# Sharing the query evacuation between ScalarE and VectorE, and recording the norm's means and the first pointwise layer later for three of four images

## The chip, the cores and the metric

The kernel runs on one core of one Trainium2 chip. The metric is the device time of one execution in microseconds (us). A core has five engines that run side by side and meet through semaphores: TensorE (PE in the profile, its weight loads PEld), VectorE (DVE), ScalarE (ACT), GpSimd (POOL) and SyncE (SP), the last used here to issue copies.

## The reference

The input is four images of 64 x 64 positions with 64 channels, in fp32. Four layers follow one another:

```python
# layer 0: self-attention over the 4096 positions of each image
q, k, v = x @ Wq + bq, x @ Wk + bk, x @ Wv + bv
x = gamma * (softmax(q k^T)^T v) + x
# layer 1: a gated convolution block
y = pw1(layernorm(x))                 # 64 -> 256 channels
y = depthwise3x3(y); y = y1 * y2      # the halves of the channels
y = y * (mean over positions of y, through sca)
x = x + pw2(y) * beta
z = pw3(layernorm(x)); x = x + pw4(z1 * z2) * gamma
# layer 2: attention of each image with itself, without projections
x = softmax(x x^T) x + x              # x.reshape(4, 64, 4096): positions and channels regrouped
# layer 3: attention with 32-channel theta, phi, g, then a batch norm over all images
x = x + batchnorm(softmax(theta phi^T) g @ W)
```

Scores, softmax and products dominate: three times four attention maps of 4096 x 4096.

## The kernel before, in words

All that matters is in `fast_path`. One image is kept as a tile X of 128 partitions by 2048 columns: the lower and the upper 64 partitions hold the 64 channels of the two halves of the positions.

**The stream.** `run` records all instructions in one order, and each engine executes its share in that order. The backbone is the list `items`: 32 items for each image's first attention (`layer0`, one item per 128 queries, images one after another, so item 32b is where image b begins), then items of `layer2` and `layer3`. An item of `layer0` is four steps of one score block (L1085, eight TensorE instructions) and one product block (L1111, eight instructions, of a tile six steps back), with one exp of 128 x 1024 (L1090) on ScalarE per score block. After a tile's four exps VectorE sums and scales (`scale`, L1098 to L1101).

**PSUM slots.** `new_ps` deals out slots of 128 x 1024 in rotation. In `layer0` two slots rotate, in `layer2` three. A block that takes a slot waits until whoever read that slot last is done. Score blocks, projections, norms and pointwise blocks all draw on the same rotation.

**Lanes.** Other work is threaded between the steps. Two lanes, `conv` and `misc`, each hold a queue of generators. After each step of `layer0` both get a tick of 1.8 units, conv first. In `layer2` an item ticks 4.6 units twice. A generator that yields a number is resumed when that many units have passed, so a yield says how much later the next piece is recorded, not how long it lasts. The `conv` lane holds `layer1(b)` from item 32b+34 on, one image after another. The `misc` lane holds `project0(b+1)` from item 32b+16 on, and later `features2`, `close2`, `open3`. The convolution work of an image takes longer than a first attention, so it runs on: that of images 2 and 3 reaches into the second attentions of images 0 and 1.

**`project0`.** For images 1 to 3 (the case "once") two query blocks and two value blocks (L1053) are recorded 3.4 units apart. A query block is eight TensorE instructions (L1027) into one slot: the lower 64 partitions get one 512-column group of each half, the upper 64 partitions the next one. ScalarE evacuates the slot in two instructions of 64 x 1024 (L1035), one for each half of the partitions, adding `bqk`. After each, SP issues a copy (L1039) of the new rows to the other 64 partitions of q.

**`norm`.** It is called twice for each image, before the first pointwise layer and before the second half of the block. It squares x on ScalarE (two ACTIVATEs of 128 x 1024, L1154), yields 4.0, takes means of x and of the squares on TensorE (16 instructions, L1160) into one slot, then on ScalarE and VectorE the variance (L1165, L1166), yields 5.0, then Ln and Exp (L1168, L1169), yields 4.0, spreads the result with eight SP copies (L1173), yields 14.0, and multiplies it into x on VectorE in two pieces (L1181), each followed by a yield of 1.8. What comes next in the lane is the first pointwise block, eight instructions a piece (L1195).

**After the norm.** `layer1` evacuates each pointwise block in two ScalarE instructions into a padded tile (`pad`, L1212), does the nine taps of the depthwise convolution on VectorE (L1226 to L1231), the channel weights (L1248), the second pointwise layer (L1257), its evacuation (L1262), again a norm, and the last two layers (L1195 again, L1274, L1276, L1280, L1281). `features2` transposes an image into one slot (L1295) and evacuates it in two halves, the lower partitions on VectorE and the upper on ScalarE (L1298). `turn` in `layer2` transposes a finished part of the output (L1349), which ScalarE (L1343) and VectorE (L1344) have put together.

Of the kernel before, what the change touches and what calls it, by code (L numbers as in the profile page):

```python
# [9 lines left out]
AF = mybir.ActivationFunctionType  # L10
# [681 lines left out]
def fast_path(ctx: ExitStack, tc: tile.TileContext, a: dict, out: bass.AP, bad):  # L692
    nc = tc.nc
    B, H, W, C = a["x"].shape
# [31 lines left out]
    def new_ps():  # L726
        if turn_of["banks"]:
            if turn_of["bank"] % turn_of["banks"] == turn_of["banks"] - 1:
                turn_of["bank"] += 1
            k = new_bank(), new_bank()  # L730
            return PS[:, 512 * k[0] : 512 * k[0] + 1024]
        s = turn_of["slots"][turn_of["ps"] % len(turn_of["slots"])]
        turn_of["ps"] += 1
        return PS[:, bass.ts(s, 1024)]
# [11 lines left out]
    def new_t(name="t"):  # L746
        return tp.tile([128, 1024], F32, tag="t", name=name)

    def new_big(name):
        return big.tile([128, 4096], F32, tag="big", name=name)  # L750
# [5 lines left out]
    act = nc.scalar.activation  # L756
# [77 lines left out]
    for nm in names64 + names32:  # L834
        n = flat[nm].shape[0]
# [31 lines left out]
    bqk = const.tile([128, 1], F32, name="bqk")  # L867
# [106 lines left out]
    def tok(x, s, j):  # L974
        return x[64 * s : 64 * s + 64, bass.ts(j, 512)]
# [41 lines left out]
    def project0(b):  # L1017
        x, m = X[:, b], im[b]
        m.q = new_big("q")
        m.v = new_big("v")[:, 0:2048].rearrange("p (t c) -> p t c", c=C)  # L1020
        once = ((0, "once"), (0, "v"), (1, "once"), (1, "v"))
        for j, w in once if b else ((0, "q"), (0, "v"), (1, "q"), (2, "q"), (1, "v"), (3, "q")):
            ps = new_ps()
            if w == "once":
                for o in range(2):
                    for s in range(2):
                        mm(  # L1027
                            ps[64 * o : 64 * o + 64, bass.ts(s, 512)], wq[64 * s : 64 * s + 64, 0:64],
                            tok(x, s, 2 * j + o), start=True, stop=True,
                        )  # L1030
                qs = m.q.rearrange("p (s n) -> p s n", s=2)
                for o in range(2):
                    own, other = slice(64 * o, 64 * o + 64), slice(64 - 64 * o, 128 - 64 * o)
                    n = bass.ts(2 * j + o, 512)
                    act(  # L1035
                        qs[own, :, n], ps[own, :].rearrange("p (s n) -> p s n", s=2),
                        AF.Identity, bias=bqk[own, :],
                    )
                    nc.sync.dma_start(out=qs[other, :, n], in_=qs[own, :, n])  # L1039
            elif w == "q":  # L1040
                for o in range(0, 128, 64):
                    for s in range(2):
                        mm(
                            ps[o : o + 64, bass.ts(s, 512)], wq[64 * s : 64 * s + 64, o : o + 64],
                            tok(x, s, j), start=True, stop=True,
                        )
                for s in range(2):
                    nc.vector.tensor_scalar_add(
                        m.q[:, 2048 * s + 512 * j : 2048 * s + 512 * j + 512], ps[:, bass.ts(s, 512)], bqk
                    )  # L1050
            else:
                for i in range(8):
                    mm(ps[:, bass.ts(i, 128)], x[:, bass.ts(8 * j + i, 128)], wv, start=True, stop=True)  # L1053
                for s in range(2):
                    nc.vector.tensor_add(
                        m.v[:, 16 * s + 8 * j : 16 * s + 8 * j + 8, :],
                        ps.rearrange("p (t s c) -> p t s c", s=2, c=C)[:, :, s, :],
                        bv.unsqueeze(1).to_broadcast([128, 8, C]),
                    )
            yield 3.4  # L1060
# [85 lines left out]
            items.append((lambda t=t: item(t), 0.0))  # L1146


    def norm(x, y):


        sq = [new_t("sq"), new_t("sq")]
        for i in range(2):
            act(sq[i], x[:, bass.ts(i, 1024)], AF.Square)  # L1154
        yield 4.0
        ps = new_ps()
        for i, src in enumerate(((x, x), (sq[0], sq[1]))):
            for j in range(4):
                c = 512 * j if i == 0 else 512 * (j % 2)
                mm(  # L1160
                    ps[32 * j : 32 * j + 32, bass.ts(i, 512)], jsel, src[j // 2][:, c : c + 512],
                    start=True, stop=True,
                )
        t = new_t()
        act(t[:, 0:512], ps[:, 0:512], AF.Square)  # L1165
        stt(t[:, 0:512], t[:, 0:512], -1.0, ps[:, 512:1024], ALU.mult, ALU.add)  # L1166
        yield 5.0
        act(t[:, 0:512], t[:, 0:512], AF.Ln, bias=eps1)  # L1168
        act(t[:, 512:1024], t[:, 0:512], AF.Exp, scale=-0.5)  # L1169
        yield 4.0  # L1170
        for j in range(4):
            for h in range(2):
                nc.sync.dma_start(  # L1173
                    out=y[64 * h : 64 * h + 64, bass.ts(j, 512)],
                    in_=t[32 * j + 16 * h : 32 * j + 16 * h + 16, 512:1024]
                    .unsqueeze(1).to_broadcast([16, 4, 512]),
                )
        yield 14.0
        for jp in range(2):
            cols = bass.ts(jp, 1024)  # L1180
            nc.vector.tensor_mul(y[:, cols], y[:, cols], x[:, cols])  # L1181
            yield 1.8

    pad = new_pad()
    nc.gpsimd.memset(pad[:, 0:PW], 0.0)
# [3 lines left out]
    def layer1(b):  # L1189
        x = X[:, b]  # L1190
# [8 lines left out]
                    )  # L1199

        y = xn.tile([128, 2048], F32, tag="xn", name="xn")
        yield from norm(x, y)
        yg = new_big("yg")
        yw = yg.rearrange("c (s q p h) -> c p q s h", s=2, p=2, h=H)
        ysum = sm.tile([128, 8], F32, tag="ysum", name="ysum")
        for r in (1, 0):
            inner = pad[:, PW + 1 : 65 * PW + 1].rearrange("c (p q s h) -> c q p s h", p=2, s=2, h=PW)
            for j in range(4):
                ps = new_ps()
# [8 lines left out]
            for j in range(4):  # L1218
                w0 = 16 * j
                y1 = new_t("y1").rearrange("p (w h) -> p w h", h=H)  # L1220
                for k in range(9):
                    o = (w0 + k % 3) * PW + k // 3
# [24 lines left out]
        ps = new_ps()  # L1247
# [6 lines left out]
        for j in range(4):  # L1254
            ps = new_ps()
# [8 lines left out]
            nc.vector.tensor_add(xs, xs, t[:, 0:512])  # L1264
            yield 3.5
        z = xn.tile([128, 2048], F32, tag="xn", name="xn")
        yield from norm(x, z)
        for j in range(4):
            t, u = new_t(), new_t("u")
            for r in range(2):  # L1270
                ps = new_ps()
# [6 lines left out]
            ps = new_ps()  # L1278
# [323 lines left out]
    for b in range(B):  # L1602
        if b:
            misc_to[len(items)] = True
        layer0(b)
        if b + 1 < B:
            gens = [load_x(i) for i in range(1, B)] if b == 0 else []
            misc_from[32 * b + 16] = gens + [project0(b + 1)]
        conv_from[32 * b + 34] = layer1(b)
# [18 lines left out]
    def run():  # L1628
        nc.scalar.preload_act_table_set("natural_log_exp_and_others")
        fold, loads, first = fold_qk(), load_x(0), project0(0)  # L1630
        next(fold)
        next(loads)
        next(fold)
        next(first)
        next(loads)
        between.append(lambda: next(loads))
        misc.add(first)
        conv_from[3] = setup()
        for i in range(max(max(due) + 1, len(items))):
            if i in misc_to:  # L1640
                misc.drain()
            if i in misc_from:
                misc.add(*misc_from[i])
            if i in conv_from:
                conv.add(conv_from[i])
            us = 1.0
            if i < len(items):
                fn, us = items[i]
                fn()
            for lane in (conv, misc):  # L1650
                lane.tick(us)
            for fn in due.get(i, []):
                fn()
            for lane in (conv, misc):
                lane.tick(us)
# [185 lines left out]
```

## Time and profile before

| What | us |
|---|---|
| median of 7 runs | 2574.38 |
| lowest and highest of them | 2573.50, 2575.95 |
| the profiled execution, its own time | 2573.91 |
| its span in the profile | 2572.1 |
| PE busy | 2535.9 |
| ACT busy | 1774.2 |
| DVE busy | 1128.6 |

A line of a timeline gives the start in us from the beginning of the span, the time from the first start to the last end, the engine, the line of the kernel, the operation, the names of output and input with their shapes, and how many instructions were merged; in brackets stands how long the engine sat idle before it and what released it. A line of the waits gives the waiting engine and line, the engine and line it waited for, then total us, number of times and the longest. The granted TensorE clock was 0.998 of full speed. On TensorE x8 is one block of eight instructions.

### The profile page before, as it was taken

How to read it: one execution, taken by the hardware profiler on the slowest of the kernel's cores; microseconds unless marked ns; L12 is line 12 of the kernel's file. 1: busy time of each engine (PE TensorE's matmuls, PEld its weight loads, DVE VectorE, ACT ScalarE, POOL GpSimd, SP SyncE). 2: the span in 40 equal slices, each digit the busy share in tenths (PEclk: the TensorE clock that was granted, in tenths of full speed). 3: DMA queues.
4: the chain of work that ended last, by engine and by line, in shares of the span. 5: the costliest groups of instructions: out<-in, count | busy, mean ns of one | idle time of the engine just before them, and what ended most of it. 6: DMA issues, size and time to landing. Idle time of an engine off the chain costs nothing.

```text
span 2572.1 us, 55249 instructions
## 1 busy us (share of the span) xinstructions
PE 2535.9 (99%) x24293; PEld 847.2 (33%) x24293; DVE 1128.6 (44%) x1292; ACT 1774.2 (69%) x2888; POOL 93.5 (4%) x142
## 2 busy tenths in 40 slices
PE   9999999999999999999999999999999999999998
PEld 3343333333333336333333321233321233321113
DVE  2010266321763227711772138810058600088996
ACT  4666766667666676666656679856689756579996
POOL 2000000000000000000000001000011000011110
PEclk9999999999999999999999999999999999999999
DMA  3000000001000100010010024310034110054444
GB/s 76 1 18 1 18 18 1 7 12 34 1 1 4 32 18 1 1 34 18 1 34 18 18 48 85 67 34 1 18 70 96 34 34 1 1 123 92 85 92 105
DMA packets 38380, 87.06 MB, mean 34 GB/s; under 512 B 5260, under 2 KB 13685, under 8 KB 38133
## 3 DMA queue, kind: packets, MB, share of 16 engines
q0 software_dynamic: 14528, 50.90, 9.6%
q1 hardware_dynamic: 22853, 30.72, 5.3%
q8 instruction: 192, 3.15, 0.5%
q10 hardware_dynamic: 752, 1.85, 0.2%
q14 instruction: 55, 0.45, 0.1%
HBM read 4.80 MB, written 4.19 MB: 3 GB/s over the span
## 4 chain that ended last, share of the span: by engine, by line
PE 92%; ACT 4%; DVE 3%; issue 1%; DMA 0%; SPq 0%; DVEq 0%; ACTq 0%
PE PS L1336 17%; PE PS L1318 17%; PE PS L1111 17%; PE PS L1085 16%; PE PS L1442 8%; PE PS L1499 8%; DVE tg L1490 3%; PE PS L1195 2%; ACT e L1453 2%; ACT e L1090 1%; PE PS L1053 1%; PE PS L1257 1%; PE PS L1280 1%; PE PS L1160 1%; PE PS L1417 1%
## 5 line engine op out<-in xcount | busy, mean ns | idle before, releaser
L1090 ACT ACTIVATE e<-PS 128x1024 f32<-128x1024 f32 x512 | 523.6, 1023 | 326.1 <-PE PS L1085 283.8
L1326 ACT ACTIVATE e<-PS 128x1024 f32<-128x1024 f32 x512 | 516.7, 1024 | 292.8 <-PE PS L1318 289.6
L1111 PE MATMUL PS<-e,vq 64*64 64x512 f32 x4096 | 539.9, 591 | 0.0
L1085 PE MATMUL PS<-X,q 64*64 64x512 f32 x4096 | 536.5, 590 | 1.8 <-DVE X L969 1.7
L1453 ACT ACTIVATE e<-PS 128x512 f32<-128x512 f32 (+2 forms) x586 | 501.3, 923 | 48.3 <-PE PS L1442 28.2
L1318 PE MATMUL PS<-ko 64*64 64x512 f32 x4096 | 469.7, 591 | 5.4 <-ACT e L1453 2.2
L1336 PE MATMUL PS<-e,X 64*64 64x512 f32 x4096 | 464.1, 591 | 0.0
L1490 DVE TENSOR_TENSOR tg<-tg,e 128x2048 f32<-128x2048 f32 x188 | 430.7, 2291 | 32.9 <-ACT e L1453 17.8
L1228 DVE SCALAR_TENSOR_TENSOR y<-pad,vec,y 128x1024 f32<-128x1024 f32 x240 | 308.1, 1284 | 8.2 <-ACT pad L1212 1.1
L1442 PE MATMUL PS<-tg,ph 32*64 32x512 f32 x4096 | 293.8, 613 | 0.1
L1499 PE MATMUL PS<-e,tg 128*32 128x512 f32 x2048 | 272.5, 604 | 0.0
L1085 PEld LDWEIGHTS PS<-X,q 64*64 64x64 f32 x4096 | 161.3, 133 | 279.2 <-issue 231.8
L1318 PEld LDWEIGHTS PS<-ko 64*64 64x64 f32 x4096 | 156.4, 132 | 293.9 <-issue 200.3
L1111 PEld LDWEIGHTS PS<-e,vq 64*64 64x64 f32 x4096 | 160.8, 133 | 272.7 <-issue 170.9
L1336 PEld LDWEIGHTS PS<-e,X 64*64 64x64 f32 x4096 | 155.4, 133 | 275.1 <-issue 271.9
L1098 DVE TENSOR_REDUCE sums<-zs 128x1 f32<-128x4 f32 x128 | 19.8, 155 | 374.3 <-ACT e L1090 374.2
L1344 DVE TENSOR_TENSOR ph<-ph,PS 128x512 f32<-128x512 f32 x16 | 11.0, 687 | 391.7 <-ACT ph L1343 391.7
L1442 PEld LDWEIGHTS PS<-tg,ph 32*64 32x64 f32 x4096 | 62.9, 129 | 217.5 <-ACT e L1453 185.2
L1499 PEld LDWEIGHTS PS<-e,tg 128*32 128x32 f32 x2048 | 41.5, 108 | 205.6 <-issue 201.6
L1326 ACT ACTIVATION_READ_ACCUMULATOR e<-PS 128x1 f32 x512 | 106.1, 207 | 0.0
L1090 ACT ACTIVATION_READ_ACCUMULATOR e<-PS 128x1 f32 x512 | 99.6, 195 | 0.1
L1470 POOL DMA_DIRECT2D xn<-e x16 | 8.8, 559 | 2139.5 <-PE PS L1442 1504.6
(196 smaller groups left out, 1013.0 us busy)
## 6 DMA issues: line engine op xcount, KB each, us to landing
xn<-e POOLq DMA_DIRECT2D x96, 512.0 KB, 5.1
xn<-t SPq DMA_DIRECT2D x64, 128.0 KB
ph<-tg SPq DMA_DIRECT2D x64, 128.0 KB
ko<-ko SPq DMA_DIRECT2D x16, 256.0 KB
xr<-in_x_dram SPq DMA_DIRECT2D x13, 256.0 KB
q<-q SPq DMA_DIRECT2D x12, 256.0 KB
out_dram<-o SPq DMA_DIRECT2D x7, 256.0 KB
out_dram<-o ACTq DMA_DIRECT2D x2, 512.0 KB
```

Of the source, the lines that this page charges most:

```text
L1085: mm(ps[64 * c : 64 * c + 64, bass.ts(r, 512)], m.q[rows_, 128 * t + 64 * c : 128 * t + 64 * c + 64], x[rows_, bass.ts(g, 512)], start=Tru ...
L1090: act(es[g // 2][:, bass.ts(g % 2, 1024)], ps, AF.Exp, bias=SHIFT0, accum_out=zs[:, g : g + 1],)
L1111: ins = mm(PS[64 * s : 64 * s + 64, 2048 + 512 * j : 2560 + 512 * j], vq[rows_, :], es[j // 2][rows_, k : k + 512], start=t == 0 and i < 2 ...
L1195: mm(ps[o : o + 64, bass.ts(s, 512)], w[64 * s : 64 * s + 64, 128 * r + o : 128 * r + o + 64], tok(src, s, j), start=True, stop=True,)
L1228: stt(y1, win, wt, y1, ALU.mult, ALU.add)
L1318: mm(ps[64 * c : 64 * c + 64, bass.ts(r, 512)], m.ko[rows_, 128 * jb + 64 * c : 128 * jb + 64 * c + 64], m.ko[rows_, bass.ts(2 * ib + r, 5 ...
L1326: act(es[n, jb], ps, AF.Exp, bias=SHIFT2, accum_out=m.zs[:, jb, ib : ib + 1])
L1336: mm(acc[r][64 * c : 64 * c + 64, :], xw[rows_, jb, :], es[n, jb][rows_, bass.ts(c, 512)], start=jb == 0, stop=jb == 31,)
L1442: mm(PS[64 * c : 64 * c + 64, bass.ts(banks[k], 512)], m.ph[32 * k : 32 * k + 32, 128 * mc + 64 * c : 128 * mc + 64 * c + 64], m.th[32 * k ...
L1453: act(e[:, 512 * lo : 512 * k], PS[:, 512 * banks[lo] : 512 * banks[lo] + 512 * (k - lo)], AF.Exp,)
L1490: nc.vector.tensor_add(esum, esum, e)
L1499: mm(st["y"][32 * k : 32 * k + 32, :], m.gx[:, i % 32, :], es[i][:, bass.ts(k, 512)], start=mc == 0, stop=i % 32 == 31,)
```

## The change

Three things are edited. In `project0` the second of the two query evacuations of a slot (upper 64 partitions) is made by VectorE as a `tensor_scalar_add` instead of a ScalarE activation; the first stays on ScalarE. `norm` takes a flag, which is true for images 0, 1 and 2: with it the yield after the squares is 6.0 instead of 4.0, and the yield after the second multiply is 3.6 instead of 1.8. Both calls of `norm` in `layer1` pass the flag. As the lane is a queue, everything behind a longer yield in the `conv` lane is recorded later too, image 3's convolution included.

```diff
                     n = bass.ts(2 * j + o, 512)
-                    act(
-                        qs[own, :, n], ps[own, :].rearrange("p (s n) -> p s n", s=2),
-                        AF.Identity, bias=bqk[own, :],
-                    )
+                    src = ps[own, :].rearrange("p (s n) -> p s n", s=2)
+                    if o:
+                        nc.vector.tensor_scalar_add(qs[own, :, n], src, bqk[own, :])
+                    else:
+                        act(qs[own, :, n], src, AF.Identity, bias=bqk[own, :])
                     nc.sync.dma_start(out=qs[other, :, n], in_=qs[own, :, n])
...
-    def norm(x, y):
+    def norm(x, y, slow):
...
-        yield 4.0
+        yield 6.0 if slow else 4.0
...
             nc.vector.tensor_mul(y[:, cols], y[:, cols], x[:, cols])
-            yield 1.8
+            yield 3.6 if slow and jp else 1.8
...
-        yield from norm(x, y)
+        yield from norm(x, y, b + 1 < B)
...
-        yield from norm(x, z)
+        yield from norm(x, z, b + 1 < B)
```

## The prediction

> **What bounds the kernel.** The page comes first, for the busy shares:
>
> ```profile
> PE 2535.9 (99%) x24293; PEld 847.2 (33%) x24293; DVE 1128.6 (44%) x1292; ACT 1774.2 (69%) x2888; POOL 93.5 (4%) x142
> ```
>
> TensorE sets the time, and the change neither adds nor removes a matmul. Only moments in which TensorE starts late can be won or lost. PE's waits from 140 to 1000 us, where images 1 to 3 are projected and most convolution work is laid into the first attention, are the whole prize there:
>
> ```profile
> PE PS L1160 <- ACT e L1090: 2.9, 4, 0.8
> PE PS L1053 <- ACT q L1035: 1.5, 2, 0.8
> PE PS L1195 <- ACT q L1035: 1.4, 2, 0.8
> PE PS L1195 <- ACT ko L1298: 0.5, 1, 0.5
> ```
>
> As matmul ends are modelled, I measure lateness between starts. Score and product blocks (L1085, L1111) follow each other every 0.86 us. A block of another shape (L1053, L1160, L1280, L1295, L1257, L1349) starts 0.11 us later even when it waits for nothing (383.80 to 384.76), and the block after it is 0.05 late. I count what goes beyond. The timeline at the first norm, and then at the second norm of the same image:
>
> ```profile
> 268.25 2.00 ACT L1154 ACTIVATE sq<-X 128x1024 f32<-128x1024 f32 x2
> 270.14 1.01 ACT L1090 ACTIVATE e<-PS 128x1024 f32<-128x1024 f32 x1
> 271.39 1.07 PE L1160 MATMUL PS<-X,jsel 128*32 128x512 f32 x8 [0.84 <-ACT e L1090]
> ```
>
> ```profile
> 498.92 1.99 ACT L1154 ACTIVATE sq<-X 128x1024 f32<-128x1024 f32 x2
> 500.81 1.01 ACT L1090 ACTIVATE e<-PS 128x1024 f32<-128x1024 f32 x1
> 501.97 1.09 PE L1085 MATMUL PS<-X,q 64*64 64x512 f32 x8
> 502.99 1.06 PE L1160 MATMUL PS<-X,jsel 128*32 128x512 f32 x8
> ```
>
> Two squares hold ScalarE for 2 us, so the next exp is late, and the mean matmuls need the PSUM slot that this exp empties. At 271.39 they stand two score blocks behind the squares and lose 1.02-0.11=0.91 us. At 502.99 they stand three behind, as it fell out there, and lose 0.05, with 0.02 at the score before. At 589, 822 and 915 (two behind) the loss is 0.76, 0.77 and 0.77: 3.25 us over five norms.
>
> The query evacuation of image 2:
>
> ```profile
> 370.74 2.23 ACT L1035 ACTIVATE q<-PS,bqk 64x1024 f32<-64x1024 f32 x2
> 372.99 1.02 ACT L1090 ACTIVATE e<-PS 128x1024 f32<-128x1024 f32 x1
> 373.02 2.05 PE L1053 MATMUL PS<-wv,X 128*128 128x128 f32 x16 [0.84 <-ACT q L1035]
> ```
>
> The score block before L1053 began at 371.14; 371.14+0.86+0.11=372.11 was due, so 0.91 is lost. So measured, the six evacuations cost: image 1 twice 0.11 at a score and 0.29 at L1053; image 2 0.91 and 0.97; image 3 0.56 at L1027, which follows L1195 with no product between, then 0.72 and 1.00. Sum 4.96 us.
>
> **The precedent.** The kernel already shares one evacuation between the engines, the transposes of `features2` (L1298):
>
> ```profile
> 870.37 1.22 DVE L1298 COPY ko<-PS 64x1024 f32<-64x1024 f32 x1 [5.69 <-PE PS L1295]
> 871.62 1.01 ACT L1298 COPY ko<-PS 64x1024 f32<-64x1024 f32 x1 [1.20 <-DVE ko L1298]
> 872.68 1.09 PE L1195 MATMUL PS<-xn,pw 64*64 64x512 f32 x8 [0.54 <-ACT ko L1298]
> ```
>
> The halves lie on different partitions, yet ScalarE starts 0.03 us after VectorE ends: one after the other, not side by side.
>
> **What the Trainium skill says.** "PSUM — Partial Sum Buffer", PSUM bank collisions: two engines must not touch one bank and 32-partition quadrant at once, reads included, while different quadrants may be; guarding by whole bank is the simple version. The trace agrees with the simple version here. The same page, Engine vs sequencer instructions: ScalarE's and VectorE's queues are strict FIFO; the exp at 270.14 behind the squares agrees. "Perfetto Trace Analysis", Tensor Engine Instruction: the end of a matmul is estimated, hence starts.
>
> **Part 1, evacuations.** Six ScalarE instructions of 1.11 us (L1035, half of twelve) go; six VectorE ones of the form 64x1024 out of PSUM come, 1.22 us each by the L1298 row (tensor_scalar is priced by that copy; L1048's 0.75 us for 512 columns would bound it at 1.5). In the built order of the changed kernel the VectorE half waits for ScalarE's semaphore alone, not TensorE's: it starts when ScalarE's half ends. The slot is free after 1.11+0.03+1.22=2.36 instead of 2.23 us, 0.13 later, while ScalarE is free 1.12 us earlier for the next exp. The SP queue's four copies per image wait 0.13 longer; queries are needed 13 or more items (about 90 us) later.
>
> Event by event, on the new TensorE order. Image 1: score, which takes the query slot, 0.10+0.13=0.23 late, then L1053 on time, since its exp no longer stands behind the second half: 0.40 becomes 0.23, twice. Image 2, first: the order is unchanged, 0.91 becomes 1.04. Second: the first pointwise block has moved out, two blocks and a product more now stand between, and the score that takes the slot, due at 381.92, finds it free at 382.10: 0.97 becomes 0.23. Image 3: L1195 no longer precedes L1027, so 0.56 goes; 0.72 becomes 1.04 (image 2's pattern), 1.00 becomes 1.13. Sum 3.90, gain 1.06 us. If L1298 underprices VectorE by 0.28, six are later by that: gain -0.6.
>
> Behind the waiting VectorE instruction stand the sums of the score tile (L1098 to L1101, 0.6 us) and taps of the convolution (1.28 us). In image 2 the sums move from 369.10 to 373.1; their vq is first used by a product at about 376.9, 3 us later. Taps need 4x1.28+0.6=5.7 of the 6.9 us that a tile takes; the two tiles with evacuations carry at most 5.7+1.3+1.2=8.2, a lag of some 2.6 us that the next tiles absorb. TensorE waits for the taps only at L1248, once per image.
>
> **Part 2, norms recorded later.** Six norms of images 0 to 2 get 2.0 more after the squares and 1.8 more before the first pointwise block. The new order has three or four exps between squares and mean matmuls in the five norms within the first attention. Three cost 0.07 (502.99); I take 0.07 for four as well. 3.25 becomes 0.35: gain 2.9 us (2.2 if the squares cost 0.2 at each). The sixth (1117) has no loss before. The later pointwise block itself waits for nothing of the norm in the trace before: its multiplies (L1181) at 290.7 and 291.8 precede the block at 297.3. That edit costs nothing, hidden by the score blocks between, and only moves the lane. DMAs of the norm (64, SP) move with it; none is passed by an issue that is late.
>
> **Part 3, all later convolution work moves** by 3.8 per norm, up to 23 lane units at the end. In the first attention one clash arises: L1195 then L1295 without a product at item 112, where the transposes wait for an exp: 0.42, then about 0.15. Before, this region lost 0.61, 0.19 and 0.13. One more shape change costs 0.16: gain 0.2.
>
> From 1000 to 1455 us four scores run in a row, and an evacuation just ahead of such a run delays its exps. Before: one pad pair ahead costs 0.2 (1027, 1214, 1223), two 0.75 (1282), transposes ahead 1.24 and 1.02 (1128, 1442), a norm's Ln and Exp behind the ph copy 0.63 (1198): 4.2 us. In the new order: one double pad 0.75; four single pads 0.8; an output block and transposes ahead 1.6 (VectorE and ScalarE halves in a row hold the third slot until 5.1 us after the product run, due 3.8; the exps give 0.3 more); two pointwise blocks and transposes ahead 1.6 by the same count; small ones 0.15; the Ln and Exp meet no ph copy: 0. Sum 4.9, loss 0.7. Three shape changes merge (L1257 with L1295 twice, with L1349 once), 3x0.16=0.5 back: loss 0.2 (range 1.7 loss to 1.2 gain). The lane ends some 15 us later than 1452 in the second attention, before the next stage takes over at about 1505, so nothing beyond is touched.
>
> **Sum** against the profiled execution (span 2572.1, its own time 2573.91, 1.8 around it): 1.06+2.9+0.2-0.2=4.0 us. Because small late starts round against me, I take 3.7. The span becomes 2568.4. The profiled execution is 0.5 under the median of the runs, 2574.38, so the median becomes 2570.7, 0.14% faster.
>
> **Rivals.** *Side by side*: the halves overlap, no wait between engines. Then the slot is free after about 1.2 us, and of 4.96 some 0.3 stays: 3.6 us more, 2567.1. For it: different partitions; against it: the 0.03 us handover at 871.6 and the built waits. *Given back in the second attention*: the moved lane meets score runs worse than counted, 2.5 us lost: 2573.2. For it: 1.24 us for one clash before; against: the clashes are few. *Slower*: VectorE's half stands behind taps at 48 and 80, so TensorE waits on slots held by a tap queue. To end 0.2% slower (5.1 us) four evacuations must lose 3.7+5.1=8.8 us, 2.2 each, nearly two taps; 2580. Against: taps wait only for pad, run ahead, and idle is what stands before VectorE's evacuations (4.16 us before L1055 at 375.18).
>
> **How the numbers follow.** Likeliest 0.65 (2569.3 to 2572.5), side by side 0.12, given back 0.17, slower 0.06. Of the likeliest, 0.11 reaches beyond 0.2% (5.1 us, below 2569.2; about what a measurement here can tell). Faster 0.11+0.12=0.23, slower 0.06, within 0.71. The range 2567.6 to 2574.2 leaves out the slower case and tails of the outer two.
>
> **What would show it.** Right: L1160's waits in the first attention fall from 2.9 to under 0.5 us; VectorE's query rows begin within 0.1 us of ScalarE's end; L1053 of images 2 and 3 still waits about 0.9 us, now for VectorE. Wrong: both query rows starting together (side by side), VectorE's late behind taps (slower), or late starts between 1000 and 1470 us adding to over 6 us (given back).

## The result, and the profile after

| | before | after |
|---|---|---|
| median, us (runs) | 2574.49 (34) | 2581.54 (14) |
| lowest and highest | 2573.20, 2578.57 | 2580.17, 2583.29 |
| profiled execution: own time, span | 2573.91, 2572.1 | 2579.98, 2578.2 |

The ratio is 1.0027, with a 95% interval of 1.0020 to 1.0033: the change makes the kernel 7 us slower, where 3.7 us faster had been forecast. Lines of the kernel after stand one higher than before from L1039 on; L1037 is VectorE's half of a query evacuation, L1039 ScalarE's.

The page of the kernel after: the busy shares, and of part 4 the shares of the chain that ended last.

```profile
PE 2539.5 (98%) x24293; PEld 846.3 (33%) x24293; DVE 1136.7 (44%) x1298; ACT 1766.5 (69%) x2882; POOL 93.5 (4%) x142
...
PE 89%; DVE 6%; ACT 3%; issue 1%; DMA 0%; SPq 0%; POOL 0%; DVEq 0%; ACTq 0%
```

Six instructions went from ScalarE to VectorE, as meant, and every engine does what it did. But VectorE has 6% of the chain; before it had 3%, and TensorE 92%. TensorE waits somewhere for VectorE where it did not.

To find the place I added up late starts: from every TensorE block to the next, the excess over the usual start-to-start time of such a block, counted where it passes 0.1 us. (The shape changes of 0.11 and 0.16 are in these sums; the prediction had taken them off.)

| Late starts, us | to 135 | first attention, 135 to 994 | second attention of images 0 and 1, from 994 to the first block of layer 3 after them (1513 before, 1518 after) | rest | sum | span |
|---|---|---|---|---|---|---|
| before | 4.7 | 13.5 | 9.2 | 22.3 | 49.8 | 2572.1 |
| after | 5.9 | 9.5 | 17.6 | 23.1 | 56.2 | 2578.2 |

The sums differ by 6.4, the spans by 6.1: the account of the profiled execution is nearly complete. That execution took less than any of the 14 timed runs (2579.98 against a median of 2581.54), so about 1 of the 7 us lost is in no profile. The first attention won 4.0, where 4.16 had been worked out (1.06 + 2.9 + 0.2). The second lost 8.4, where 0.2 had been. The outer columns differ by 1.2 and 0.8; over all kernels here they vary from 4.7 to 5.9 and from 22.3 to 25.1, in no order that follows the edits. The rest, the last stretch of the kernel, follows the clock, as the last section shows.

The first attention first. PE's waits of the kernel after, from 140 to 1000 us:

```profile
PE PS L1054 <- DVE q L1037: 2.0, 2, 1.0
PE PS L1196 <- DVE q L1037: 1.0, 1, 1.0
PE PS L1296 <- ACT e L1091: 0.4, 1, 0.4
```

The norms' 2.9 us (L1160 before) are gone. What stays is the wait for a query slot, and now it is VectorE that holds it. The timeline at image 2's first query evacuation:

```profile
371.18 1.10 ACT L1039 ACTIVATE q<-PS,bqk 64x1024 f32<-64x1024 f32 x1
...
372.31 1.29 DVE L1037 TENSOR_SCALAR q<-PS,bqk 64x1024 f32<-64x1024 f32 x1 [4.22 <-ACT q L1039]
...
373.65 0.60 PE L1054 MATMUL PS<-wv,X 128*128 128x128 f32 x3 [1.02 <-DVE q L1037]
```

VectorE had been idle for 4.22 us, and starts 0.03 us after ScalarE's end (371.18 + 1.10 = 372.28), released by it, as the bracket says. The halves run one after the other, and the slot is free 2.42 us after the first began, 0.19 later than the 2.23 before.

Now the second attention. PE's waits of the kernel after from 1000 to 1470 us; before, this list held L1298 for 1.1 us and an exp for 0.4:

```profile
PE PS L1319 <- DVE tg L1397: 4.3, 1, 4.3
PE PS L1319 <- ACT ko L1299: 1.9, 2, 1.0
PE PS L1319 <- ACT e L1327: 1.0, 1, 1.0
PE PS L1393 <- DVE X L1373: 0.2, 1, 0.2
```

The first line is a wait that the kernel before did not have. It happens once. The timeline of the kernel after around it:

```profile
1284.40 1.91 PE L1393 MATMUL PS<-X,thw 64*32 64x512 f32 x12
...
1286.51 1.05 PE L1393 MATMUL PS<-X,thw 64*32 64x512 f32 x4 [0.20 <-DVE X L1373]
1287.49 1.95 PE L1319 MATMUL PS<-ko 64*64 64x512 f32 x16
1287.70 0.81 DVE L1227 TENSOR_SCALAR y<-pad,vec 128x1024 f32<-128x1024 f32 x1
1288.54 3.92 DVE L1229 SCALAR_TENSOR_TENSOR y<-pad,vec,y 128x1024 f32<-128x1024 f32 x3
...
1292.38 1.28 DVE L1397 TENSOR_SCALAR tg<-PS,vec 128x1024 f32<-128x1024 f32 x1
...
1293.72 3.33 PE L1319 MATMUL PS<-ko 64*64 64x512 f32 x16 [4.28 <-DVE tg L1397]
```

The theta matmuls of image 0 (L1393, in `open3`) fill a slot, and VectorE is to empty it into `tg` (L1397). But VectorE executes in order, and ahead of it stand taps of image 3's convolution (L1227, L1229: 0.81 and 3.92 us). The evacuation starts 4.89 us after the score block that follows the theta matmuls (1287.49 to 1292.38), and the third score block of the run, which takes the slot, starts at 1293.72 instead of 1289.26, two halves of a block after 1288.40. The kernel before at the same point:

```profile
1293.61 3.67 PE L1318 MATMUL PS<-ko 64*64 64x512 f32 x32
1293.82 1.28 DVE L1396 TENSOR_SCALAR tg<-PS,vec 128x1024 f32<-128x1024 f32 x1 [7.35 <-PE PS L1392]
...
1295.02 0.80 DVE L1226 TENSOR_SCALAR y<-pad,vec 128x1024 f32<-128x1024 f32 x1
```

There such taps came just after theta: VectorE stood idle for 7.35 us and began to empty the slot 0.21 us after the first score block had begun, and the four score blocks ran through. The order of these two on VectorE's queue was turned round by the lane that moved.

One more part of the cost is seen in the same place. After the wait the 16 matmuls take 3.33 us, twice the 1.7 of two score blocks. The table of stretches of the kernel after (stretch, length, busy time and count of PE, PEld, DVE, ACT and POOL, then the granted TensorE clock, DMA share, GB/s):

```profile
1288.00:1290.00 2.00, 1.44 (x16) 0.28 (x8) 1.93 (x3) 1.29 (x3) 0.00 (x0) 1.00 0.00 0
...
1294.00:1296.00 2.00, 2.00 (x12) 0.51 (x11) 1.97 (x2) 0.23 (x1) 0.00 (x0) 0.50 0.00 0
...
1297.00:1298.00 1.00, 1.00 (x21) 0.16 (x17) 0.50 (x1) 0.88 (x1) 0.00 (x0) 1.00 0.00 0
```

The clock stood at half in the stretch after the wait. The page "TensorE: Matmul & The Clock Gate" of the Trainium skill, What's actually happening, says that TensorE's clock falls to half after an idle window of about 3.4 us and returns after about as long a busy one. The trace agrees: 4.9 us passed between two starts, and then four groups of matmuls started 0.91, 0.85 and 0.85 us apart where 0.43 is usual. So the block that waited was 4.46 us late, and the first block after the run 6.0 (1296.98 instead of 1288.40 + 3 x 0.86 = 1290.98): a wait of 4.5 cost 6.

### The profile page after: what moved, and what is told of

It reads as the page before. It is cut to its first block, busy times and chain, and to the rows that moved or that the text cites. A ratio compares the mean times of both kernels' runs of the same rounds, so it can differ in the third digit from the quotient of the medians.

```text
span 2578.2 us, 55243 instructions
## 1 busy us (share of the span) xinstructions
PE 2539.5 (98%) x24293; PEld 846.3 (33%) x24293; DVE 1136.7 (44%) x1298; ACT 1766.5 (69%) x2882; POOL 93.5 (4%) x142
## 4 chain that ended last, share of the span: by engine, by line
PE 89%; DVE 6%; ACT 3%; issue 1%; DMA 0%; SPq 0%; POOL 0%; DVEq 0%; ACTq 0%
PE PS L1112 17%; PE PS L1086 17%; PE PS L1337 17%; PE PS L1319 16%; PE PS L1443 8%; PE PS L1500 7%; DVE tg L1491 3%; PE PS L1196 2%; ACT e L1454 2%; DVE y L1229 1%; PE PS L1054 1%; PE PS L1281 1%; PE PS L1258 1%; PE PS L1161 1%; PE PS L1418 1%
## 5 line engine op out<-in xcount | busy, mean ns | idle before, releaser
L1327 ACT ACTIVATE e<-PS 128x1024 f32<-128x1024 f32 x512 | 516.7, 1024 | 301.4 <-PE PS L1319 298.2
L1229 DVE SCALAR_TENSOR_TENSOR y<-pad,vec,y 128x1024 f32<-128x1024 f32 x240 | 308.0, 1283 | 10.2 <-ACT pad L1213 3.2
```

Source lines behind the costliest of these rows:

```text
L1229: stt(y1, win, wt, y1, ALU.mult, ALU.add)
L1327: act(es[n, jb], ps, AF.Exp, bias=SHIFT2, accum_out=m.zs[:, jb, ib : ib + 1])
```

## Experiments

Three theories. **A**: the loss is image 0's theta evacuation, which the moved lane put behind image 3's taps on VectorE. **B**: VectorE's half of the query evacuation costs it, directly or through what is queued behind. **C**: many small clashes of the moved lane with score runs add up. Each kernel was timed beside the kernel before on its own chip, whose medians were 2574.45, 2574.91 and 2574.30 in the three sets; ratios are against these.

### The change in two: the query evacuation alone, the norms alone

The first has the query edit and the yields of before, the second the two longer yields and the evacuation of before.

```diff
+                    if o:
+                        nc.vector.tensor_scalar_add(qs[own, :, n], src, bqk[own, :])
+                    else:
+                        act(qs[own, :, n], src, AF.Identity, bias=bqk[own, :])
```

> Kernel before with the shared query evacuation alone. Theory A (the loss of 7 us comes from theta's evacuation in open3 of image 0 standing behind image 3's taps on VectorE, because the longer yields moved the taps there): the lane is not moved, theta's evacuation stands where it was, so about the time of before, 2573.5 to 2576 us, and the wait of the score block for theta is absent. Theory B (the VectorE half of the query evacuation itself costs the 7 us, through slots held longer): 2579 us or more. Theory C (the many small clashes of moved convolution work with score runs, none dominant): as A, 2573.5 to 2576.

> Kernel before with the longer yields alone, both query halves on ScalarE. Theory A and C: the loss is all here, 2579 to 2582 us, with the score block of the second attention waiting some 4 us for theta's evacuation. Theory B: faster than before by the norm's 2.9 us, about 2571.5 us.

The query edit alone: 2575.84, ratio 1.0005 (0.9996 to 1.0013), no difference that can be told. Late starts in the first attention 14.2 against 13.5, in the second 9.3 against 9.2. The norms alone: 2579.81, ratio 1.0019 (1.0011 to 1.0027); late starts 9.1 and 18.9, and this among PE's waits from 1000 to 1470 us:

```profile
PE PS L1318 <- DVE tg L1396: 4.3, 1, 4.3
```

B falls: the wait and the loss come with the yields alone, and without the query edit. The query edit gains nothing alone.

### Theta of image 0 on ScalarE

The kernel after with one evacuation moved off VectorE.

```diff
-        nc.vector.tensor_scalar_add(m.th, ps, V("L3_conv_theta_b"))
+        act(m.th, ps, AF.Identity, bias=V("L3_conv_theta_b")) if b == 0 else nc.vector.tensor_scalar_add(m.th, ps, V("L3_conv_theta_b"))
```

> Changed kernel with image 0's theta evacuation moved from VectorE to ScalarE, where no taps stand in the queue; nothing else differs. Theory A: 5 to 6 us come back, 2575.5 to 2577 us, and the wait of 4.3 us is gone. Theory C: at most 2 us come back, 2579.5 us or more. Theory B: no change, 2581 us.

2574.27, ratio 0.9996 (0.9988 to 1.0005): 7.3 us below the kernel after by the medians, 4.6 by the profiled spans (its profiled run took 2575.45, the most of its 13), and late starts of the second attention down from 17.6 to 11.8. The timeline there:

```profile
1287.19 3.66 PE L1319 MATMUL PS<-ko 64*64 64x512 f32 x32
1287.31 1.12 ACT L1397 ACTIVATE tg<-PS,vec 128x1024 f32<-128x1024 f32 x1 [4.88 <-PE PS L1393]
1287.40 0.80 DVE L1227 TENSOR_SCALAR y<-pad,vec 128x1024 f32<-128x1024 f32 x1
```

The same taps stand on VectorE at the same time, and the four score blocks run through in 3.66 us. A holds: the loss goes with this one evacuation, and more comes back than the 5 to 6 us expected. But the interval has 1 in it: without the wait the change is no slower than before, and no faster either, though the first attention keeps its 4.0 us. The 2.6 us of late starts over before that stay include 1.23 before the score at 1287.19, where theta's last matmuls wait for a piece of X that VectorE makes behind two other taps (A's pattern a second time), and clashes on ScalarE: squares ahead of a score run (1.43), two runs with transposes ahead (1.6 each, against 1.35 and 1.13 before; with the shape changes, which the prediction's 1.24 and 1.02 leave out). In this profile another 1.9 us over before are late in the last stretch, where the clock halved once, at 2473.5 us.

### The same delay made without moving anything

The kernel before, with theta of image 0 evacuated five times over, so that its slot comes free four evacuations later. Nothing else is moved or added.

```diff
+        for _ in range(5 if b == 0 else 1):
             nc.vector.tensor_scalar_add(m.th, ps, V("L3_conv_theta_b"))
```

> Kernel before with image 0's theta evacuation made five times in a row on VectorE (same values into the same place), so that its slot is freed 4 x 1.28 = 5.1 us later, with no other change. Theory A: the slot has almost no slack, TensorE loses 4 to 5.5 us, 2578.5 to 2580 us. If a late theta were hidden by other work, as theories B and C need: 2574.5 to 2576 us.

2582.55, ratio 1.0029 (1.0018 to 1.0039), with 16.3 in place of 9.2 in the second attention. The timeline:

```profile
1293.68 1.95 PE L1318 MATMUL PS<-ko 64*64 64x512 f32 x16
1293.89 6.56 DVE L1397 TENSOR_SCALAR tg<-PS,vec 128x1024 f32<-128x1024 f32 x5 [7.36 <-PE PS L1392]
...
1300.51 1.98 PE L1318 MATMUL PS<-ko 64*64 64x512 f32 x8 [4.88 <-DVE tg L1397]
```

The third score, due at 1295.4, waited until 1300.51. The slot has no slack at all: the delay reached the end in full and more, 7.0 us of late starts for 5.1 of delay, and 8.1 us by the medians. The clock explains the excess of late starts here too: it stood at 0.50 from 1300 to 1303 us. I had expected 4 to 5.5 us, without the clock.

### How far the lane moves

The kernel before with one of the two yields for three images, or with both for fewer images. Each puts the convolution work of image 3 at another place against `open3(0)`. Of the lines below the first two are one kernel each; the last two are one kernel each too, with both yields.

```diff
+        yield 6.0 if slow else 4.0
+            yield 3.6 if slow and jp else 1.8
...
+        yield from norm(x, y, b < 1)
+        yield from norm(x, y, b < 2)
```

> Kernel before with the yield of 6.0 after the squares alone (five norms stand ahead of image 3's first taps' end, so the lane is 10 to 12 units late there instead of 19 to 23), queries as before and 1.8 after the multiply. Theory A: theta's evacuation follows the last tap of one tile and no new tile's taps, so the wait is shorter, 1 to 3 us instead of 4.3, and the time lies between, 2573 to 2577 us. Theory C: no step at theta; the time follows the clashes, anything from 2571 to 2579 us.

> Kernel before with the yield of 3.6 after the second multiply alone, queries and means as before: the part that gains nothing in the first attention, 9 to 10.8 units later at image 3. Theory A: theta waits 2.5 to 4 us as with yield6_only and nothing is won, 2579 to 2582 us. Theory C: within 2 us of before.

> Kernel before with both longer yields for image 0 only, queries as before: image 3's convolution is recorded 7.6 units later (19 to 23 in the changed kernel). In the new VectorE order theta's evacuation follows the last taps of one channel half, as with yield6_only, but these end some 11 us earlier than there would have to be for the full shift. Theory A: theta finds VectorE free or nearly so, waits under 1.5 us, and the time is 2572.5 to 2575.5 us (0.9 us are won at image 0's norm). Theory C: no step, the time is anything within 2572 to 2578 us, with no theta wait.

> Both longer yields for images 0 and 1, queries as before: 15.2 units later at image 3. Theory A: taps are still queued when theta's block is done, the wait is 3 to 4.5 us and the time 2577 to 2580 us, as with the full change. Theory C: no step, no theta wait, 2572 to 2578 us.

| Kernel | lane later in the end by, units | median, us | ratio | late in the first attention, us | in the second | wait for theta |
|---|---|---|---|---|---|---|
| image 0 alone | 7.6 | 2575.48 | 1.0001 (0.9993 to 1.0010) | 11.3 | 10.5 | none |
| 3.6 alone | 10.8 | 2582.76 | 1.0030 (1.0020 to 1.0041) | 13.3 | 17.4 | 2.2 |
| 6.0 alone | 12.0 | 2579.63 | 1.0015 (1.0008 to 1.0022) | 10.4 | 17.4 | 3.6 |
| images 0 and 1 | 15.2 | 2580.58 | 1.0020 (1.0011 to 1.0030) | 9.8 | 19.1 | 4.9 |
| norms alone | 22.8 | 2579.81 | 1.0019 (1.0011 to 1.0027) | 9.1 | 18.9 | 4.3 |

Of the two kernels from which little harm was expected one is a hit; the other is a miss in size: 12.0 met a wait of 3.6 us, not 1 to 3. The two from which harm was expected are small misses: images 0 and 1 waited 4.9 us where at most 4.5 were expected, 3.6 alone 2.2 where at least 2.5 were, and both took 0.6 to 0.8 us longer than the range. With 7.6 the taps clear VectorE just in time:

```profile
1289.06 1.41 DVE L1231 SCALAR_TENSOR_TENSOR yg<-pad,vec,y 128x512 f32<-128x512 f32 x2
...
1290.63 1.28 DVE L1396 TENSOR_SCALAR tg<-PS,vec 128x1024 f32<-128x1024 f32 x1 [0.16 <-PE PS L1392]
```

Theta starts 0.16 us after VectorE is free, so some tenths more and it would wait. The loss doesn't grow with the distance; what counts is which taps stand ahead when theta comes. With 3.6 alone the wait is the shortest and the time the longest: late starts at theta are 4.2, the clock's part included, and another 2.8 come at 1120 us, where the squares of a norm fall between its own mean matmuls, which there follow a score run:

```profile
1122.05 2.02 ACT L1154 ACTIVATE sq<-X 128x1024 f32<-128x1024 f32 x2
1123.18 2.00 PE L1160 MATMUL PS<-sq,jsel 128*32 128x512 f32 x8 [1.62 <-ACT sq L1154]
```

So C has a share in that kernel, and A alone doesn't order these times.

### The gain kept, the phase given back

The kernel before with the means 2.0 later, and the yield of 14.0 ahead of the multiplies shortened by as much, so that whatever follows a norm stays where it was.

```diff
-        yield 4.0
+        yield 6.0 if slow else 4.0
...
-        yield 14.0
+        yield 12.0 if slow else 14.0
```

> Kernel before with the norm's means recorded 2.0 units later in images 0 to 2, and these 2.0 taken back from the yield of 14.0 behind the norm's copies, so that the lane behind each norm stays where it was; queries as before. Theory A: the gain of the first attention without the loss of the second, 2.5 to 3 us, 2571 to 2572.5 us. If recording the means later were itself the cause: 2576 us or more.

2571.76, ratio 0.9988 (0.9981 to 0.9994), with 10.6 and 9.3 of late starts: the 2.9 us of the norms are won and kept, with no theta in PE's waits.

### The query slot divided by PSUM bank

The kernel before with each query evacuation divided otherwise: each engine takes both halves of the partitions, but only one of the two banks of the slot (a bank, as the kernel uses the word, is 512 of its 1024 columns), in pieces of 64 x 512.

```diff
-                    act(
-                        qs[own, :, n], ps[own, :].rearrange("p (s n) -> p s n", s=2),
-                        AF.Identity, bias=bqk[own, :],
-                    )
+                    src = ps[own, :].rearrange("p (s n) -> p s n", s=2)
+                    act(qs[own, 0, n], src[:, 0], AF.Identity, bias=bqk[own, :])
+                    nc.vector.tensor_scalar_add(qs[own, 1, n], src[:, 1], bqk[own, :])
```

> Kernel before with each query slot evacuated by both engines, but divided by PSUM bank instead of by partition half: ScalarE takes the first bank (two pieces of 64x512), VectorE the second. Norms as before. If the handover between the engines comes from both reading one bank, the halves now run side by side, the slot is free after some 1.4 us and 3 to 4.5 of the 4.96 us of late starts go: 2570 to 2571.5 us. If the engines still take turns, or the taps hold VectorE's half: 2574 to 2576 us.

2570.71, ratio 0.9985 (0.9978 to 0.9992); late starts of the first attention from 13.5 to 9.8. (Its profiled run, 2573.44, lies above the median; the clock halved twice in its last stretch.) The timeline at image 2's first query evacuation:

```profile
369.95 1.53 DVE L1037 TENSOR_SCALAR q<-PS,bqk 64x512 f32<-64x512 f32 x2 [2.52 <-PE PS L1027]
...
370.06 1.38 ACT L1036 ACTIVATE q<-PS,bqk 64x512 f32<-64x512 f32 x2
...
371.49 1.86 PEld L1052 LDWEIGHTS PS<-wv,X 128*128 128x128 f32 x16 [0.87 <-ACT q L1036]
371.49 2.05 PE L1052 MATMUL PS<-wv,X 128*128 128x128 f32 x16
```

VectorE is released by TensorE, not by ScalarE, and the two overlap: the slot is empty 1.5 us after the first began, and the value block shows no wait. The gain that the change sought from two engines is there once the division is by bank. What makes the halves of the changed kernel take turns is a wait that is built into the program, VectorE's for ScalarE. No run left that wait out with the division by partitions, so whether the two engines could read the two partition halves side by side stays open.

### The two together, and a third evacuation

First both of the last two edits. Then with them the evacuation in `features2` (L1298), which the kernel before divides by partitions, divided by bank as well.

```diff
-            for e, copy in enumerate((nc.vector.tensor_copy, nc.scalar.copy)):
+            for e in range(2):
...
+                for h, copy in enumerate((nc.vector.tensor_copy, nc.scalar.copy)):
+                    copy(
+                        kv[own, bass.ts(2 * g + h, 4), e, :],
+                        ps[own, bass.ts(h, 512)].rearrange("p (a n) -> p a n", n=128),
+                    )
```

> The two edits of means_later and q_banks together on the kernel before. If their gains are independent, the sum: 6 to 7.5 us, 2567 to 2568.5 us. If they feed on the same idle time: not under 2570 us.

> The kernel both with the evacuation of features2 divided by PSUM bank too, ScalarE and VectorE side by side instead of in turn. The score runs behind these transposes were late by 1.24 and 1.02 us in the second attention, and blocks in the first by 0.61, 0.19 and 0.13. If taking turns is what makes them late: 1.5 to 2.5 us under both, 2567.5 to 2568.5 us. If the four smaller pieces cost what the overlap gives: as both, 2569 to 2570.5 us.

Both: 2569.78, ratio 0.9976 (0.9967 to 0.9985), just under the 2570 of the second expectation, and short of the sum. Late starts of the first attention add up (6.8, so 6.7 won for 2.9 and 3.7 alone), the medians do not: 5.1 us instead of 3.1 + 4.2. The profile of both has 2.2 us more late starts in the last stretch than that of before; the clock halved there once, at 2469.1 us, and not in the profile of before. How much of the difference of the medians this explains is left open.

With the third: 2565.37, ratio 0.9961 (0.9947 to 0.9975), 9 us faster than before and 16 faster than after; span 2564.9, late starts 5.9 in the first attention and 7.0 in the second (6.8 and 9.3 without it). That is 4.4 us for the third edit by the medians (3.8 if each is taken against the kernel before of its own set), 3.8 by the spans, 3.2 by late starts in the two attentions, where I had expected 1.5 to 2.5. Its timeline at a slot of transposes, where the prediction showed halves one after the other:

```profile
873.04 1.18 ACT L1298 COPY ko<-PS 64x512 f32<-64x512 f32 x2 [0.47 <-PE PS L1294]
873.21 1.40 DVE L1298 COPY ko<-PS 64x512 f32<-64x512 f32 x2
```

Both work at once, and the slot is empty after 1.57 us (873.04 to 874.61), where 2.26 us had passed before (870.37 to 872.63).

## Why the prediction was wrong

**Right: the norms.** 3.25 us were to become 0.35. Measured by the same count: 0.13, 0, 0, 0 and 0.05. The gain of 2.9 is there, and stays in the kernel with the phase given back.

**Right: the query evacuations run one after the other.** The handover of 0.03 us was read from L1298 of the kernel before, and is the one seen at 372.31. Event by event: image 1 0.35 twice (0.23 forecast); image 2 1.28 and 0.35 (1.04, 0.23); image 3 1.05 and 1.16 (1.04, 1.13), and nothing at L1027. The sum is 4.5 instead of 3.9, in part because VectorE took 1.29 us instead of 1.22; so 0.4 us were won instead of 1.06. *Side by side* did not happen. Different partitions, which the prediction counted in its favour, were not enough in the program as it was built; different banks were.

**Right: the first attention's clash** at item 112, 0.64 instead of 0.57.

**Wrong: Part 3, the second attention, "loss 0.2".** The clashes that the prediction listed there came out near their sizes: the double pad 0.92 (0.75), the single pads 1.4 for five of them (0.8 for four), the two runs with transposes ahead 1.6 and 1.63 (1.6 each). These make 5.5 instead of 4.9, with shape changes, which the forecast took off. But the list counted only what the moved lane does to ScalarE and to the lane's own slots, and one clash on ScalarE was missed (squares ahead of a score run at 1398, 1.43). The step that failed is the sentence of Part 1 carried into Part 3, that "TensorE waits for the taps only at L1248". That is so for the taps' results. It says nothing of other work on VectorE's queue that holds a PSUM slot. `open3(0)` is in the other lane and was not moved; so it was not looked at. Image 3's taps moved in front of its theta evacuation, and of a piece of X that theta needs: 6.0 + 1.23 = 7.2 us. Take them from the 17.6 of late starts, and 10.4 is left against 9.2: by this sum the loss without the one oversight would have been some 1.2, within the range given for it (1.7 loss to 1.2 gain). No run shows that. The nearest, theta of image 0 on ScalarE, takes away the 6.0 but not the 1.23, and ends level with the kernel before instead of 3.7 us faster. The changed order of the two on VectorE could have been read from the built order before the run.

**The rival *Slower* had the mechanism and the wrong place.** It said a slot held by a tap queue, and looked for it at the query evacuations, where VectorE is indeed idle (4.22 us before L1037). The argument against it, that taps wait only for pad and run ahead, holds there, and fails at theta: VectorE had worked without a pause since 1256.68 us when theta's evacuation came, and the taps ahead of it read a pad that ScalarE had last filled at 1243.6. The taps did not wait for pad; VectorE was far behind. *Given back in the second attention* named the stretch and its bound of over 6 us was passed, with another cause and three times the loss.

**Size of the wait.** Even had the wait been seen, its price would have been read as 4.3 or 4.5 us. It cost 6.0, since the clock halved.

## What to carry to other kernels

When work moves in a recorded order, list for each engine that it uses what it is moved past, also of lanes that were not touched: an evacuation behind a queue of long vector work holds its slot, and TensorE pays for it without needing any of that vector work. A delay that is wanted in one place can be taken back in the next yield, so that nothing downstream changes its phase. Two engines that share an evacuation are to be given different PSUM banks: divided by partitions they ran in turn here, divided by bank together. And where the profiles of two kernels differ by a few us, look at the granted clock of each stretch before the difference is put down to an edit.

## What the runs showed of the hardware

**A wait of TensorE can halve its clock, and the price depends on when it falls.** The granted clock stood at 0.50 after the waits for theta, and TensorE ran groups 0.86 instead of 0.43 us apart. In the clock records of all 14 profiles every change after the first comes a whole number of steps of 3.413 us after it (in the kernel after the clock falls after 375 steps, 1280.0 us), wherever the wait lies. So one wait has more than one price. In the kernel after and in the one with the norms alone TensorE waits the same 4.28 us for theta, with 4.89 between starts; the clock is at half for 3.41 us in the first and for 6.83 in the second, and the block of L1417 (L1418 after) behind it starts 6.0 us late in the first and 7.2 in the second.

With 3.6 alone even a gap of 2.84 us between starts was enough, as the table of stretches of that kernel shows:

```profile
1292.00:1295.00 3.00, 3.00 (x24) 0.77 (x22) 2.94 (x3) 0.96 (x3) 0.00 (x0) 1.00 0.00 0
1295.00:1298.00 3.00, 0.77 (x12) 0.07 (x6) 2.85 (x4) 2.03 (x4) 0.00 (x0) 1.00 0.00 0
1298.00:1301.00 3.00, 3.00 (x20) 0.97 (x24) 0.00 (x0) 1.11 (x2) 0.00 (x0) 0.58 0.00 0
```

That is shorter than the idle window of 3.4 us of which the Trainium skill's page "TensorE: Matmul & The Clock Gate" speaks; TensorE had done 0.77 us of work within these 3 us, and the clock fell all the same.

In the last stretch, where TensorE waits several times for VectorE's `tg`, a gap between starts of 2.3 us halved the clock in one profile and not in another. The timeline of the kernel before, and then of the one with the query slot divided by bank, with a line of its table of stretches:

```profile
2401.07 1.57 PE L1442 MATMUL PS<-tg,ph 32*64 32x512 f32 x16
2404.34 1.07 PE L1511 MATMUL PS<-tg,ones 128*32 128x512 f32 x8 [1.71 <-DVE tg L1490]
```

```profile
2397.51 1.57 PE L1441 MATMUL PS<-tg,ph 32*64 32x512 f32 x16
2400.80 1.94 PE L1510 MATMUL PS<-tg,ones 128*32 128x512 f32 x8 [1.72 <-DVE tg L1489]
```

```profile
2400.80:2403.80 3.00, 3.00 (x16) 0.65 (x16) 0.94 (x2) 0.38 (x1) 1.11 (x2) 0.50 0.44 161
```

Counted as in the table of late starts (a recount, 0.6 lower throughout), the last stretch has 21.7 to 22.5 us in the seven profiles in which the clock does not halve there, 23.5 to 23.9 in the five with one halving and 24.1 to 24.5 in the two with two. That is up to 2.8 us of span from a stretch that no edit touches.

**Division by bank.** 64 x 1024 by partitions: 1.10 and 1.29 us in turn, 2.42 together. In 64 x 512 by bank: 1.38 on ScalarE and 1.53 on VectorE for two pieces each, at once, 1.5 together. The turn in the first case is the built program's wait, not shown to be a need of the hardware.
